# Layer 1's own rows scattered by rank in layer 0 and loaded plainly, in a four-layer graph network on one core

## The chip, the cores and the metric

The kernel runs on one core of one Trainium2 chip. Times are device microseconds (us) of that core. The core has five engines that run side by side, each with its own in-order queue: TensorE (PE, matrix products and transposes), VectorE (DVE), ScalarE (ACT), GpSimd (POOL) and SyncE (SP, which here only issues transfers). ACT and SP issue plain transfers; POOL issues the indirect ones, gathers and scatters whose row numbers lie in memory. An engine that waits for a semaphore holds back everything behind it in its own queue.

## The reference, cut to what matters

There are N = 2708 nodes with 128 features each, and a 2708 x 2708 adjacency matrix in which some 16 entries per row are not zero. Four layers follow one another, each ending in a residual sum and a layer norm. Layers 0 and 1 matter here:

```python
# layer 0
msg = H.T @ X;  inv_deg = 1 / H.sum(axis=0)          # H = adj
x = layernorm(x + msg * inv_deg[:, None])
# layer 1
s = x @ msg_w[:, :D].T
d = x @ msg_w[:, D:].T
messages = gelu(s[:, None, :] + d[None, :, :] + msg_b)
aggregated = einsum('ijd,ij->id', messages, adj)
h = gelu(concat([x, aggregated]) @ upd_w.T + upd_b) + x
x = layernorm(x + layernorm(h))
```

Layer 2 is `adj @ (x @ W)` with a norm over the nodes, layer 3 an attention over the neighbours in four heads.

## The kernel before

The nodes form 22 blocks of 128 rows (the last has 20). Since the matrix is sparse, layer 1 and layer 3 don't work on it whole but on lists: per node up to 31 neighbours with their values, and the node's own entry of the diagonal.

**First stage, making the lists.** SP loads the rows of adjacency, 1354 KB per block, into a ring of nine buffers (`load`, L388). For each block PE accumulates layer 0's product (`count_and_sum`, L400), then POOL clears the diagonal entry in the tile, ACT counts the entries (a Sign pass with accumulation, L416), and DVE finds the entries, segment by segment, with 8-wide maximum and index searches (`extract`, L420). Four weights of layer 1 are loaded and transposed at L679 (`weight`, L369), after nine blocks have been taken in the program's order.

`lists` (L514) decodes what the search found. A found place is a number of which the low 8 bits are the column within a segment, and the bits above, counted backwards, the candidate's number. The decoding makes columns and values of it, on DVE, and copies the count, the node number and the diagonal beside them.

**Ranks.** Nodes are then sorted by their count of neighbours, so that blocks of 128 sorted nodes have lists of like length (`CAPS`, L44: 30 messages for the first block down to 8). There are two groups: blocks 0 to 12 and blocks 13 to 21. `ranking(g)` (L478) makes a key per node, transposes it, writes it to DRAM, reads it back broadcast to all partitions, and lets ACT run one Sign pass per block whose accumulated sum says how many keys are greater. `ranked(g)` (L507) turns the sums into row numbers on DVE. `place` (L546) scatters the lists by these ranks to `lists_dram`, and `sorted_lists` (L558) loads them back in sorted order, with `perm`, the node that stands at each sorted place, and `idx`, the neighbours' row numbers.

**Layer 0's end.** `layer0` (L722) normalises four blocks at a time (five such quads, and two single blocks), as a pipeline of generators that yield between steps. It leaves `x` in `xs`, multiplies it by the weight of `d`, and writes `x` and `d` in natural node order to the two halves of `dx_dram`, 256 floats a row, with two plain transfers on SP per quad.

**Layer 1.** For each sorted block, in the order `TURNS`, `own_row` (L808) gathers the block's own rows of `dx_dram` by `perm`, one block ahead, into `x_s`, of which there are three buffers. `messages` (L816) computes `s` from it, and for each list position gathers 128 rows of 512 bytes (`msg`, L844), seen as a table of twice as many half rows, which is why `idx` is doubled at L569. DVE adds `s`, ACT applies Gelu, DVE weighs and sums. There are five `msg` buffers of up to eight positions. `update` (L860) finishes the block; L881 is the last that reads `x_s`. Its result is scattered to `x2_dram`.

Beside this, blocks 13 to 21 are still searched, and all blocks are transposed (`transposed`, L898): PE transposes, ACT copies to `at_sb` (three buffers), SP writes to `at_dram`. From the twelfth block on, layer 2's product takes rows of `at_dram`, gathered by `perm` (`layer2`, L942). `load3` (L577) loads lists for layer 3 on SP, and `spread` (L597) lays them out.

**What sets the order.** A planner orders each engine's instructions and puts in all waits; program order is the priority. Up to L799 DVE keeps the order in which the program is written (`manual_schedule`); later work may be put between. Each queue is then fixed, and runs as its waits allow.

```python
            x_s = mine.tile([P, 2, D], FP, name="x_s", bufs=3)
            gather(
                x_s[0:n].rearrange("p t d -> p (t d)"), dx_dram, perm[0:n, b : b + 1]
            )
```

Of the kernel before, what the change touches and what calls it, by code (L numbers as in the profile page):

```python
# [9 lines left out]
FP = mybir.dt.float32  # L10
AF = mybir.ActivationFunctionType
ALU = mybir.AluOpType
# [73 lines left out]
def gnn_resnorm_kernel(  # L86
# [124 lines left out]

    dx_dram = tables.tile([NBLK * P, 2 * D], FP, name="dx_dram")
# [30 lines left out]
    def gather(dst, table, index, rows=N):  # L243
        nc.gpsimd.indirect_dma_start(  # L244
            out=dst,
            out_offset=None,
            in_=table[0:rows, :],
            in_offset=bass.IndirectOffsetOnAxis(ap=index, axis=0),
        )
# [84 lines left out]
    with ExitStack() as layer:  # L334
# [22 lines left out]
        nc.gpsimd.iota(places_i, pattern=[[-256, CAND]], base=256 * CAND, channel_multiplier=0)  # L357
# [11 lines left out]
        def weight(src, name):  # L369
            raw = small.tile([P, P], FP, name="raw_w")  # L370
            nc.scalar.dma_start(raw, src)
# [142 lines left out]
        def lists(b0, b1):  # L514
# [8 lines left out]
            nc.vector.tensor_copy(rows[:, :, 2 * SLOTS], cnt[:, b0:b1])  # L523
            nc.vector.tensor_copy(rows[:, :, 2 * SLOTS + 1], node[:, b0:b1])
            nc.vector.tensor_copy(rows[:, :, 0], diag[:, b0:b1])
            nc.vector.tensor_copy(rows[:, :, SLOTS], node[:, b0:b1])
            nc.vector.tensor_copy(code, k2[:, b0:b1, 0 : SLOTS - 1])
            nc.vector.tensor_scalar(low, code, 255, None, ALU.bitwise_and)
            nc.vector.tensor_scalar(seg, code, 8, None, ALU.arith_shift_right)
            nc.vector.tensor_scalar(seg, seg, -1.0, float(CAND), ALU.mult, ALU.add)  # L530
            nc.vector.tensor_scalar(seg, seg, 3, None, ALU.arith_shift_right)
            nc.vector.tensor_scalar(seg, seg, float(NSEG - 1), 0.0, ALU.min, ALU.max)
            cols = rows[:, :, SLOTS + 1 : 2 * SLOTS]
            nc.vector.scalar_tensor_tensor(cols, seg, float(SEGW), low, ALU.mult, ALU.add)
            nc.vector.tensor_scalar(cols, cols, float(N - 1), 0.0, ALU.min, ALU.max)
            nc.vector.scalar_tensor_tensor(cols, v1, 0.0, cols, ALU.is_gt, ALU.mult)
            nc.vector.tensor_scalar(
                seg, seg, float(SPAN), float(127 - TOP), ALU.mult, ALU.add
# [19 lines left out]
        def sorted_lists(g):  # L558
# [3 lines left out]
            for c0, c1, n in parts:  # L562
# [6 lines left out]
                nc.vector.tensor_scalar(  # L569
                    idx[0:n, c0:c1, :], ls[0:n, c0:c1, SLOTS : 2 * SLOTS], 2.0, None, ALU.mult  # L570
                )
# [150 lines left out]
        def layer0(b0, count, n):  # L722
# [31 lines left out]
            nc.vector.reciprocal(v, v)  # L754
            for j in range(count):
                nc.vector.tensor_scalar(
                    xs[0:n, b0 + j, :], h[0:n, j, :], sums[:, j : j + 1], v[:, j : j + 1],
# [3 lines left out]
            nc.sync.dma_start(  # L761
                dx_dram[b0 * P : b0 * P + w, D : 2 * D].rearrange("(b p) w -> p b w", p=n),
# [1259 lines left out]
```

## Time and profile before

| what | value |
|---|---|
| median of 3 runs | 1965.46 us (1963.5 to 1975.81) |
| the profiled execution | 1612.16 us, span 1610.4 us |
| mean granted PE clock in it | 0.708 |
| busy PE, DVE, ACT, POOL (of the span) | 73%, 73%, 43%, 56% |
| own-row gathers (`x_s`), POOL | 22, 950 ns each |
| message gathers (`msg`), POOL | 368, 950 ns each |
| gathers of `at_dram`, POOL | 22, 948 ns each |

The profile is of one execution, the table's median of three others. A row of the profile gives the line in the kernel, the engine, the operation, what it writes and reads, how often it ran, its busy time and mean duration, and then the engine's idle time just before it with what ended that. "issue" means that the profile shows no releaser.[...] In the page, the span falls into making the lists (to about 170 us), layer 0's end (to about 205 us), layers 1 and 2's product (to about 840 us), the norm and tables (to about 905 us), and layer 3.

### The profile page before, as it was taken

The numbers are of one execution on the slowest core, as the hardware profiler recorded it, in microseconds if no ns is written. First come the engines' busy times: TensorE is split into PE (matmuls) and PEld (weight loads), VectorE is DVE, ScalarE is ACT, GpSimd is POOL, SyncE is SP. The second block draws the span as 40 slices with busy tenths as digits, with TensorE's granted clock in tenths as the row PEclk, the third lists the DMA queues.
The fourth block names the chain that finished last, engine by engine and source line by source line (L and its number), as shares of the span: only waits on it lengthen the run. The fifth ranks groups of instructions, "written<-read, shape, count | busy, mean of one in ns | idle before, by whom it ended". The sixth has DMA issues, their size and how long they took to land. (4 is left out here: it accounts for less than half of the span.)

```text
span 1610.4 us, 23528 instructions
## 1 busy us (share of the span) xinstructions
PE 1170.0 (73%) x5771; PEld 827.4 (51%) x5771; DVE 1182.0 (73%) x5376; ACT 697.6 (43%) x2670; POOL 897.8 (56%) x996
## 2 busy tenths in 40 slices
PE   6996333555357536666896689988888988998994
PEld 6896323344246435565783234544554545555553
DVE  7999967888356554444547398897888888888883
ACT  3448467655235311111115244544444555455442
POOL 1001167777667577765613577665656656676521
PEclk9898655655556677677678766776787778767675
DMA  8733368888358734343333779875766766877630
GB/s 273 286 141 127 94 186 201 246 248 237 101 136 215 224 77 164 128 169 140 104 109 121 245 229 225 234 223 159 221 204 198 209 187 166 230 199 215 186 92 8
DMA packets 164685, 288.21 MB, mean 179 GB/s; under 512 B 46610, under 2 KB 118512, under 8 KB 157439
## 3 DMA queue, kind: packets, MB, share of 16 engines
q0 software_dynamic: 60496, 190.76, 40.9%
q1 hardware_dynamic: 95923, 90.91, 18.1%
q10 hardware_dynamic: 8120, 4.95, 1.2%
q8 instruction: 48, 0.79, 0.2%
q14 instruction: 98, 0.80, 0.2%
HBM read 242.50 MB, written 43.97 MB: 178 GB/s over the span
## 5 line engine op out<-in xcount | busy, mean ns | idle before, releaser
L244 POOL DMA_INDIRECT g<-t_dram,idx x400 | 403.6, 1009 | 189.3 <-issue 141.1
L244 POOL DMA_INDIRECT msg<-dx_dram,idx x368 | 349.7, 950 | 119.1 <-issue 93.9
L1314 ACT ACTIVATE sum_junk<-g 126x128 bf16<-126x128 f32 (+3 forms) x800 | 235.2, 295 | 115.8 <-DVE g L1306 63.4
L1283 PE MATMUL z<-x,copies 32*126 32x512 f32 (+3 forms) x800 | 210.8, 875 | 33.1 <-DVE g L1483 32.3
L949 PE MATMUL acc<-x_nat,at_rows 128*128 128x128 f32 (+2 forms) x968 | 151.0, 319 | 83.1 <-DMA at_rows<-at_dram,perm 82.7
L923 PE MATMUL pt_a<-ident,rows 128*128 128x128 f32 (+2 forms) x475 | 110.1, 388 | 133.6 <-ACT at_sb L928 132.3
L949 PEld LDWEIGHTS acc<-x_nat,at_rows 128*128 128x128 f32 (+2 forms) x968 | 138.0, 226 | 93.2 <-DMA at_rows<-at_dram,perm 75.9
L1483 DVE TENSOR_TENSOR g<-g,z 126x1536 f32<-126x1536 f32 (+3 forms) x100 | 174.8, 1748 | 11.7 <-PE z L1283 11.2
L1288 PE MATMUL z<-g,ident 126*126 126x512 f32 (+3 forms) x200 | 164.7, 918 | 0.0
L923 PEld LDWEIGHTS pt_a<-ident,rows 128*128 128x128 f32 (+2 forms) x475 | 80.2, 200 | 156.4 <-ACT at_sb L928 152.6
L1314 ACT ACTIVATION_READ_ACCUMULATOR sum_junk<-g 126x1 f32 (+3 forms) x800 | 149.5, 187 | 0.0
L835 DVE SCALAR_TENSOR_TENSOR own<-msg,ls,own 128x128 f32<-128x128 f32 (+1 forms) x302 | 105.4, 349 | 56.1 <-ACT msg L853 53.5
L1360 PEld LDWEIGHTS po_s<-wm,g 126*128 126x128 f32 (+3 forms) x800 | 118.6, 232 | 42.1 <-DVE wm L1347 32.7
L1360 PE MATMUL po_s<-wm,g 126*128 126x24 f32 (+6 forms) x800 | 120.5, 305 | 25.0 <-DVE wm L1347 23.3
L405 PE MATMUL acc<-x_nat,rows 128*128 128x129 f32 (+3 forms) x1012 | 130.5, 291 | 11.2 <-DMA rows<-in_adj_dram 11.2
L405 PEld LDWEIGHTS acc<-x_nat,rows 128*128 128x128 f32 (+2 forms) x1012 | 125.2, 201 | 16.2 <-DMA rows<-in_adj_dram 11.7
L1306 DVE SCALAR_TENSOR_TENSOR g<-g,a_ps 126x1024 f32<-126x1024 f32 (+3 forms) x100 | 121.1, 1211 | 0.0
L435 DVE MAX8 cv<-rows 128x8 f32<-128x247 f32 (+2 forms) x242 | 95.5, 400 | 6.7 <-POOL rows L395 6.7
L1288 PEld LDWEIGHTS z<-g,ident 126*126 126x126 f32 (+3 forms) x200 | 40.6, 254 | 116.3 <-issue 89.7
L1283 PEld LDWEIGHTS z<-x,copies 32*126 32x126 f32 (+3 forms) x800 | 63.7, 239 | 70.6 <-DVE g L1483 27.0
L430 DVE FIND_INDEX8 ci<-cv,rows 128x8 uint32<-128x247 f32 (+2 forms) x242 | 98.4, 407 | 0.0
L1298 DVE SCALAR_TENSOR_TENSOR g<-z,a 126x128 f32<-126x128 f32 (+3 forms) x400 | 91.7, 284 | 2.3 <-PE z L1288 0.9
(297 smaller groups left out, 2093.2 us busy)
## 6 DMA issues: line engine op xcount, KB each, us to landing
rows<-in_adj_dram SPq DMA_DIRECT2D x34, 1354.0 KB
at_dram<-at_sb SPq DMA_DIRECT2D x105, 256.0 KB
g<-t_dram,idx POOLq DMA_INDIRECT x400
msg<-dx_dram,idx POOLq DMA_INDIRECT x368
t_dram<-t_row SPq DMA_DIRECT2D x21, 256.0 KB
at_dram<-at_sb SPq DMA_DIRECT2D x21, 64.0 KB
dx_dram<-x_nat SPq DMA_DIRECT2D x5, 256.0 KB
dx_dram<-d_sb SPq DMA_DIRECT2D x5, 256.0 KB
```

The source lines that it names most:

```text
L244: nc.gpsimd.indirect_dma_start(out=dst, out_offset=None, in_=table[0:rows, :], in_offset=bass.IndirectOffsetOnAxis(ap=index, axis=0),)
L405: nc.tensor.matmul(accs0[k][0:m, c0 : c0 + f1 - f0], lhsT=rows[0:n, j0 : j0 + m], rhs=x_nat[0:n, b, f0:f1], start=k not in started, stop=( ...
L430: nc.vector.max_index(out=ci[0:n, at], in_max=cv[0:n, at], in_values=rows[0:n, c0 : c0 + cw])
L835: nc.vector.scalar_tensor_tensor(to, m, v, last, ALU.mult, ALU.add)
L923: nc.tensor.transpose(pt[0:m, j, 0:n], rows[0:n, c0 : c0 + m], ident[0:n, 0:n])
L949: nc.tensor.matmul(accs2[ib // 4][0:m, (ib % 4) * D : (ib % 4 + 1) * D], lhsT=at[0:n, i0 : i0 + m], rhs=xw[0:n, b, :], start=(k == 0 and i ...
L1283: nc.tensor.matmul(z3[0:e, r, :] if r < 3 else z1[0:e], lhsT=copies[g][rows, j, :], rhs=own[b][1][rows, :], start=True, stop=r < 3, skip_g ...
L1288: nc.tensor.matmul(z1[0:e], lhsT=ident[0:e, 0:e], rhs=g4[0:e, 3, 0:HD], start=False, stop=True, skip_group_check=True,)
L1306: nc.vector.scalar_tensor_tensor(z, z, 0.0, a_ps[0:e].unsqueeze(1).to_broadcast((e, 2, HD)), ALU.max, ALU.mult)
L1314: nc.scalar.activation(junk[0:e], g4[0:e, r, hd * D : (hd + 1) * D], AF.Identity, accum_out=sc[0:e, r, hd : hd + 1],)
L1360: nc.tensor.matmul(po[:, p0 * HEADS : (p0 + g) * HEADS], lhsT=g4s[i][0:e, r, HD : HD + D], rhs=wm[0:e, 4 * i + r, :, :], start=True, stop= ...
L1483: nc.vector.tensor_tensor(z, z, z3[0:e], ALU.add)
```

## The change

- `layer0` writes its result into a new tile `dx`, which holds `d` and `x` of a node side by side, three buffers for quads and two for single blocks. It no longer writes `xs`. `d` alone goes to a new table `d_dram` in natural order, by a plain transfer on SP; `d` and `x` together are scattered by rank to `dx_dram`, 128 rows of 1 KB per scatter, 22 in all, declared independent of one another.
- For that, `ranking(1)` moves ahead of layer 0 and `ranked(1)` into its middle. A quad that reaches beyond block 12 waits for it before it scatters.
- `own_row` becomes a plain load on SP, since `dx_dram` is now in sorted order. Messages are gathered from `d_dram`; `idx` isn't doubled any more.
- `lists`: the offset of the places is chosen so that one shift by 11 gives the segment; 16 operations on DVE become 9, and four small copies go to ACT.
- The four layer-1 weights are loaded on SP's queue, not on ACT's.

```diff
+    d_dram = tables.tile([NBLK * P, D], FP, name="d_dram")
...
-        nc.gpsimd.iota(places_i, pattern=[[-256, CAND]], base=256 * CAND, channel_multiplier=0)
+        nc.gpsimd.iota(places_i, pattern=[[-256, CAND]], base=256 * (CAND + 7), channel_multiplier=0)
...
             raw = small.tile([P, P], FP, name="raw_w")
-            nc.scalar.dma_start(raw, src)
+            nc.sync.dma_start(raw, src)
...
-            nc.vector.tensor_copy(rows[:, :, 2 * SLOTS], cnt[:, b0:b1])
-            nc.vector.tensor_copy(rows[:, :, 2 * SLOTS + 1], node[:, b0:b1])
-            nc.vector.tensor_copy(rows[:, :, 0], diag[:, b0:b1])
-            nc.vector.tensor_copy(rows[:, :, SLOTS], node[:, b0:b1])
+            for at, of in ((0, diag), (SLOTS, node), (2 * SLOTS, cnt), (2 * SLOTS + 1, node)):
+                nc.scalar.copy(rows[:, :, at], of[:, b0:b1])
             nc.vector.tensor_copy(code, k2[:, b0:b1, 0 : SLOTS - 1])
             nc.vector.tensor_scalar(low, code, 255, None, ALU.bitwise_and)
-            nc.vector.tensor_scalar(seg, code, 8, None, ALU.arith_shift_right)
-            nc.vector.tensor_scalar(seg, seg, -1.0, float(CAND), ALU.mult, ALU.add)
-            nc.vector.tensor_scalar(seg, seg, 3, None, ALU.arith_shift_right)
-            nc.vector.tensor_scalar(seg, seg, float(NSEG - 1), 0.0, ALU.min, ALU.max)
+
+            nc.vector.tensor_scalar(seg, code, 11, None, ALU.arith_shift_right)
             cols = rows[:, :, SLOTS + 1 : 2 * SLOTS]
-            nc.vector.scalar_tensor_tensor(cols, seg, float(SEGW), low, ALU.mult, ALU.add)
-            nc.vector.tensor_scalar(cols, cols, float(N - 1), 0.0, ALU.min, ALU.max)
+            nc.vector.scalar_tensor_tensor(cols, seg, float(-SEGW), low, ALU.mult, ALU.add)
+            nc.vector.tensor_scalar(
+                cols, cols, float(NSEG * SEGW), float(N - 1), ALU.add, ALU.min
+            )
...
             nc.vector.reciprocal(v, v)
+            dx = brief.tile([P, count, 2, D], FP, name=f"dx{count}", bufs=3 if count > 1 else 2)
             for j in range(count):
                 nc.vector.tensor_scalar(
-                    xs[0:n, b0 + j, :], h[0:n, j, :], sums[:, j : j + 1], v[:, j : j + 1],
+                    dx[0:n, j, 1, :], h[0:n, j, :], sums[:, j : j + 1], v[:, j : j + 1],
                     ALU.add, ALU.mult,
                 )
             w = (count - 1) * P + n
-            nc.sync.dma_start(
-                dx_dram[b0 * P : b0 * P + w, D : 2 * D].rearrange("(b p) w -> p b w", p=n),
-                xs[0:n, b0 : b0 + count, :],
-            )
             yield
...
-            d_sb = brief.tile([P, 4, D], FP, name="d_sb")
-            nc.scalar.copy(d_sb[0:n, 0:count], pm[0:n, 0:count])
+            nc.scalar.copy(dx[0:n, :, 0, :], pm[0:n, 0:count])
             nc.sync.dma_start(
-                dx_dram[b0 * P : b0 * P + w, 0:D].rearrange("(b p) w -> p b w", p=n),
-                d_sb[0:n, 0:count],
-            )
-
+                d_dram[b0 * P : b0 * P + w, :].rearrange("(b p) w -> p b w", p=n),
+                dx[0:n, :, 0, :],
+            )
+            while b0 + count > SPLIT and 1 not in known:
+                yield
+            for j in range(count):
+                did = scatter(
+                    dx_dram, rank[0:n, b0 + j : b0 + j + 1],
+                    dx[0:n, j].rearrange("p t d -> p (t d)"),
+                )
+                for before in known[1:]:
+                    tc.declare_no_dep(
+                        did, before, query=mybir.DependencyQuery.ANY_SYNC,
+                        reason="each row has a place of its own",
+                    )
+                known.append(did)
+
+
+        known = [0]
         running = []
+        ranking(1)
         for quad in [(NFULL, 1, NREM), *quads()[:-1]]:
             running.append(layer0(*quad))
             for steps in reversed(list(running)):
                 if next(steps, "done") == "done":
                     running.remove(steps)
+        ranked(1)
+        known[0] = 1
         while running:
...
         sorted_lists(0)
-        ranking(1)
...
             x_s = mine.tile([P, 2, D], FP, name="x_s", bufs=3)
-            gather(
-                x_s[0:n].rearrange("p t d -> p (t d)"), dx_dram, perm[0:n, b : b + 1]
+            nc.sync.dma_start(
+                x_s[0:n],
+                dx_dram[b * P : b * P + n, :].rearrange("p (t d) -> p t d", t=2),
             )
...
-                    gather(
-                        msg[0:n, k, :], dx_dram.rearrange("n (t d) -> (n t) d", t=2),
-                        idx[0:n, b, c0 + k + 1 : c0 + k + 2], rows=2 * N,
-                    )
+                    gather(msg[0:n, k, :], d_dram, idx[0:n, b, c0 + k + 1 : c0 + k + 2])
...
-                    if e == SPLIT:
-                        ranked(1)
```

## The prediction

> **What bounds the kernel now.** I read the stretches of 25 us first: VectorE (DVE) is full from 25 to 175 us, GpSimd (POOL) from 205 to about 810 us, TensorE (PE) and DVE together after 925 us. The change acts in the first two. Next came the groups by line; the columns are busy us, mean ns of one, then the engine's idle time before them and what ended it.
>
> ```profile
> L244 POOL DMA_INDIRECT msg<-dx_dram,idx x368 | 349.7, 950 | 119.1 <-issue 93.9 <-DMA msg<-dx_dram,idx 8.4 <-ACT back L908 2.9
> L244 POOL DMA_INDIRECT x_s<-dx_dram,perm x22 | 20.9, 950 | 65.1 <-issue 36.3 <-ACT junk L502 27.6 <-PE pt_a L923 0.6
> L252 POOL DMA_INDIRECT lists_dram<-lists,rank x22 | 21.5, 978 | 20.4 <-DVE spread L604 6.0 <-issue 5.2 <-DVE deg L706 4.8
> ```
>
> One gather takes 0.95 us and POOL starts the next 0.30 us later. A full POOL therefore shows 19 busy us in 25, and that is what the stretches from 225 to 400 us and from 575 to 700 us show (17.0 to 19.1). Layer 1 is paced by POOL at 1.25 us per gather. The own-row gathers are few but have much idle time ahead of them. The timelines of POOL and of DVE show where it lies:
>
> ```profile
> 705.59 0.94 POOL L244 DMA_INDIRECT at_rows<-at_dram,perm  x1 [0.30 <-issue]
> 706.84 1.00 POOL L252 DMA_INDIRECT x_dram<-x_n,perm  x1 [0.30 <-DVE spread L604]
> 708.14 0.96 POOL L244 DMA_INDIRECT at_rows<-at_dram,perm  x1 [0.30 <-issue]
> 717.39 0.92 POOL L244 DMA_INDIRECT x_s<-dx_dram,perm  x1 [8.29 <-issue]
> ...
> 747.19 0.95 POOL L244 DMA_INDIRECT x_s<-dx_dram,perm  x1 [7.42 <-issue]
> ```
> ```profile
> 716.27 0.29 DVE L881 SCALAR_TENSOR_TENSOR new<-new,x_s 128x128 f32<-128x128 f32 x1 [1.91 <-ACT new L880]
> ...
> 746.15 0.29 DVE L881 SCALAR_TENSOR_TENSOR new<-new,x_s 128x128 f32<-128x128 f32 x1 [1.92 <-ACT new L880]
> ```
>
> Each stalled own-row gather starts about 1 us after L881, the last reader of an older `x_s`. Of three buffers none is free, and POOL, which works in order, stands with the next block's messages queued behind. It is a ring: POOL's `at_rows` gathers, their landing, PE's products ahead of the update's, L881, POOL again. Such stalls stand at 561.95 (6.65 us), 717.39 (8.29), 747.19 (7.42) and 772.53 (9.64), together 32.0 us.
>
> The start, in the timelines of PE, POOL and DVE:
>
> ```profile
> 15.21 0.45 PE L373 MATMUL pt_w<-ident,raw_w 128*128 128x128 f32 x1 [15.21 <-DMA raw_w<-in_L_gnn_msg_w_dram]
> 16.16 0.29 POOL L395 TENSOR_SCALAR_AFFINE_SELECT rows<-rows 128x128 f32<-128x128 f32 x1 [11.97 <-DMA lnw<-in_L_gnn_ln_w_dram]
> 16.49 0.74 DVE L435 MAX8 cv<-rows 128x8 f32<-128x247 f32 x2 [6.70 <-POOL rows L395]
> ```
>
> PE's first instruction is the transpose of a weight, issued on ScalarE's (ACT's) queue at 11.12 us behind the features. The products of block 0, the clearing of its diagonal and DVE's search all stand behind it. Last, the waits (us in total, times, longest), of SyncE's queue (SP) and of DVE:
>
> ```profile
> SPq L583 <- DMA lists_dram<-lists,rank: 29.7, 1, 29.7
> ...
> DVE to L619 <- DMA node<-lists_dram: 27.1, 2, 25.6
> ```
>
> SP works in order too: from 412.9 to 442.6 us it stood at one load, and DVE stood 25.6 us for another behind it. This matters because the change gives SP more to wait for.
>
> **The Trainium skill.** "DMA: Bandwidth & Descriptors", section "Queues, rings and completion order": on each DMA engine a queue's descriptors are consumed in ring order, and the engine alternates between queues. So a weight on SP's queue comes behind the adjacency rows issued before it; no row of this trace shows a weight there. The same page, "Anatomy of one DMA — SWDGE (gpsimd) path": a DMA's semaphore wait is spent on the sequencer that issues it, and a DMA has about 2.0 us of fixed cost. The trace agrees: the write of `key_dram` is issued at 197.78 us and the read that waits for it at 200.20. "Perfetto Trace Analysis", section "DMA Instruction — SWDGE (GPSIMD)": POOL's interval is descriptor generation, not the movement of data. It agrees: a gather of 10.8 KB rows (`at_rows`, 0.948 us) costs POOL what one of 512-byte rows does (0.950).
>
> **Part by part.** The profiled execution took 1612.16 us, of which 1610.4 are span. The median of the runs is 1965.46, 353 us longer, and nothing in the page shows where. I sum against 1612.16 and carry the result to the median in microseconds, unscaled, since POOL and queues pace what changes. (Scaled by 1.219 it would be a fifth more.)
>
> *Weights on SP's queue.* The four loads leave ACT. On SP they come after nine row loads, so I expect their transposes to fall behind the products of those blocks on PE. PE then starts when rows 0 and the first features are in. DMA moved 2.3 MB by 8 us (43, 256, 414 and 418 GB/s in four stretches of 2 us) and 3.0 MB by 10; two row tiles and three feature blocks are 3.0 MB, so about 10 us. DVE's own set-up ends at 9.8. DVE starts near 10.3 instead of 16.49: -6 us. DVE is full up to 175 us, so this goes through. Bounds: -7; and +22 if the weight stays first on PE but lands behind nine row tiles of 1.39 MB (12.5 MB at 321 GB/s, the mean of the first 60 us, is 39 us). The later two loads wait on SP for a free raw buffer, about to 65 us, with row loads queued behind them. Today the tenth is issued at 38.3 and its search begins near 98, so I cost that at nothing.
>
> *Lists in nine operations.* Per call three integer operations go (starts 150.35 to 151.28, 0.93 us) and four small copies move to ACT (149.17 to 149.45, 0.28 us). That is 1.2 us for seven blocks and about 0.9 for six: -2.1 us on full DVE before layer 0. The two later calls lie under POOL's pace: nothing. ACT gets 0.8 us per call (four at 0.19, the row of `var`); the lists' scatters wait for that, and their reload isn't used before 194 us. The changed base of the codes and the plain index copy cost nothing.
>
> *Ranking group 1 early.* Nine Sign passes of 1044 columns (1.17 + 0.19 us, 12.1 us in all) move from 204 to 226 us, where they lay under POOL's gathers, into layer 0. The chain is key at 174, write and broadcast about 7 us, passes from 181. ACT had 6.3 us of idle time from there to 200.5: +5.8 us if nothing else stretched. DVE stands at `ranked(1)` for the last pass, with the normalising of quads queued behind.
>
> *Scatters by rank.* 22 scatters at 1.27 us (the row of `lists_dram`) are 28 us of POOL time, in a stretch where POOL idles from 178 to 205. Seven plain writes on SP go. But the new tile `dx4` has three buffers for five quads, and a buffer is free only when its scatters have landed. The first quad's `d` is copied at 188.5; four scatters are 5.1 us, landing 2: 195.6, where the fourth quad's scaling starts at 190.46 today. The second: 192.6, POOL busy until 198.7, landed 200.7, where the fifth quad's scaling starts at 192.43: +8.3 us. DVE waits in order, layer 1's searches behind it. The passes partly overlap these waits. I take +11 us for both until the first message gather (208.0 us today), POOL's remaining scatters included. Bounds: +6 and +20.
>
> *Own rows on SP.* Two of the 22 gathers stood ahead of the first message and are inside that +11. Eleven up to 530 us at 1.25 us are 13.8; DVE is 85% busy there and DMA 0.8 to 0.9, so I take -10 (0 to -14). Nine later: -11.3. The slot stalls leave POOL. PE is then next late: 16.1 and 13.7 busy us in 25 between 700 and 750 are 18 in a cycle of 29.8, against POOL's 21. I take half, -16 (0 to -31). The plain loads are issued one block ahead; five message buffers hold some 40 gathers, 50 us, which hides a late own row. If that cover is gone, POOL stands as before. Message gathers from `d_dram` read the same 512-byte rows: nothing.
>
> Sum: -6 - 2.1 + 11 - 10 - 11.3 - 16 = -34.4 us. The profile would be 1578 us, the median 1931 us.
>
> **Rivals.** *The gain is hidden.* Layer 0 costs +20 (passes and buffers added), and PE's wait for `at_rows` (82.7 us in nine waits) replaces the slot stalls: -6 - 2 + 20 - 10 - 11 is -9, so 1956. For it: those waits are there already. Against it: they end sooner when POOL issues sooner.
>
> *SP stands in line: slower.* Own-row loads wait on SP for an `x_s` buffer, and the first for all 22 scatters. Behind them stand the `at_dram` writes and adjacency loads. With writes late, the three `at_sb` buffers fill, ACT stops in its copies (it waits 32.6 us for those writes today), Gelu and L881 come later, and so does the buffer. Price: 5 us in each of 12 blocks before 530 us, +60 - 34 = +26: 1991. It decides from 2.9 us per block (34/12). For it: the 29.7 us stand. Against it: SP mostly waits for ACT at its writes (152 us), so it has slack.
>
> *The weight stays first on PE:* +22 in place of -6, so -6 in all: 1959. Against it: nine row loads of the same queue arrive before it.
>
> **Numbers.** Likeliest 0.55: 1931, its own range 1905 to 1946. Hidden 0.20: 1956. SP 0.18: 1991. Weight 0.07: 1959. About 1% (19.7 us) is what a measurement of this kernel can tell from no change. Of the likeliest, 0.53 are faster by over 1%; of hidden and weight, 0.05, and 0.03 are slower. Faster 0.58, same 0.24, slower 0.18. Range 1902 to 1985: up to half of SP's case, and the low end is the sum with all slot stalls gone and the first half in full.
>
> **What would show it.** Right: DVE's first MAX8 near 10 us; POOL's own-row gathers gone and no idle over 5 us between the block's last `at_rows` and the next message; first message gather near 211 us (219 less the 8 before it). Wrong: pt_w still PE's first; SP's waits at the own-row load over 3 us per block with writes behind; POOL still idle 7 us per block late in layer 1, now for something else.

## The result and the profile after

Beside each other on one chip, the kernel before took 1971.90 us (median of 12 runs, 1963.50 to 1982.36) and the changed one 1974.23 us (12 runs, 1964.51 to 1983.05). The ratio is 0.9992, 95% interval 0.9968 to 1.0016: no difference. Forecast were 1931 us, a ratio of 0.982.

One thing has to be known for all numbers that follow: the time of this kernel depends on the chip. On some chips the kernel before takes about 1625 us (I call them short), on others about 1970 us (long); the profile of before was taken on a short chip, the runs of both kernels and the profile of after on long ones. A ratio is therefore always to the kernel before on the same chip, and stages are compared between profiles of the same sort of chip.

The profiled execution of the changed kernel took 1977.24 us, of which 1975.5 are span. Its start, from the timeline of all engines (start, duration, engine, line, what, and in brackets the idle time before it and what ended it):

```profile
10.91 9.29 PE L406 MATMUL acc<-x_nat,rows 128*128 128x129 f32 x66 [10.91 <-DMA x_nat<-in_x_dram]
...
12.08 0.74 DVE L436 MAX8 cv<-rows 128x8 f32<-128x247 f32 x2 [2.27 <-POOL rows L396]
```

The weights' transpose is no longer PE's first instruction, and DVE's search begins at 12.08 us in place of 16.49. The other end of the start, POOL's timeline:

```profile
170.38 0.96 POOL L253 DMA_INDIRECT lists_dram<-lists,rank  x1 [0.30 <-issue]
196.90 0.96 POOL L253 DMA_INDIRECT dx_dram<-dx,rank  x1 [25.57 <-ACT dx L773]
198.16 0.96 POOL L253 DMA_INDIRECT dx_dram<-dx,rank  x1 [0.30 <-DVE k L467]
...
227.01 0.96 POOL L253 DMA_INDIRECT dx_dram<-dx,rank  x1 [0.30 <-issue]
230.94 0.98 POOL L245 DMA_INDIRECT msg<-d_dram,idx  x1 [2.97 <-DVE ka L471]
```

POOL still idles to 196.90, then runs all 22 scatters in a row, and only behind the last of them gathers its first message, at 230.94 us. It did that at 208.00 before. What kept POOL idle stands in ACT's timeline:

```profile
177.04 1.17 ACT L503 ACTIVATE junk<-key_row,nkey 128x1044 int8<-128x1044 f32 x1
178.11 0.18 ACT L503 ACTIVATION_READ_ACCUMULATOR junk<-key_row,nkey 128x1 f32 x1
178.21 0.38 ACT L743 ACTIVATE ln_junk<-h,sums 128x128 bf16<-128x128 f32 x1
178.50 0.19 ACT L743 ACTIVATION_READ_ACCUMULATOR ln_junk<-h,sums 128x1 f32 x1
178.59 1.15 ACT L503 ACTIVATE junk<-key_row,nkey 128x1044 int8<-128x1044 f32 x1
...
196.03 0.59 ACT L773 COPY dx<-pm_d 128x512 f32<-128x512 f32 x1
```

The nine Sign passes of the early ranking (L503) lie one by one between the Squares of the first quads (L743), so the first full quad's `d` is copied at 196.03 us. Behind 230.94 us the profiles of before and after can't be compared, since they are of two sorts of chip. The groups by line of after show what the long chip does:

```profile
L245 POOL DMA_INDIRECT msg<-d_dram,idx x368 | 348.0, 946 | 266.5 <-issue 209.7 <-ACT at_sb L936 41.2 <-ACT back L916 10.4
...
L253 POOL DMA_INDIRECT x_dram<-x_n,perm x22 | 21.9, 994 | 134.0 <-DVE own L846 64.3 <-DVE x_n L319 52.4 <-DVE spread L601 14.3
...
L253 POOL DMA_INDIRECT dx_dram<-dx,rank x22 | 21.2, 963 | 35.4 <-ACT dx L773 25.6 <-issue 4.9 <-DVE kb L460 3.8
```

A message gather costs POOL what it did (946 ns), but there are 266.5 us of idle time before them, and 134.0 before the scatters of the updates, which wait for DVE. The own-row gathers are gone, and 22 scatters of nearly the same price (963 ns) have come.

### The profile page after: what moved, and what is told of

The parts are those of the page before. It is cut to its first block, busy times and chain, and to the rows that moved or that the text cites. A ratio compares the mean times of both kernels' runs of the same rounds, so it can differ in the third digit from the quotient of the medians.

```text
span 1975.5 us, 23576 instructions
## 1 busy us (share of the span) xinstructions
PE 1274.4 (65%) x5771; PEld 887.3 (45%) x5771; DVE 1190.2 (60%) x5348; ACT 701.0 (35%) x2686; POOL 894.6 (45%) x996
## 5 line engine op out<-in xcount | busy, mean ns | idle before, releaser
L245 POOL DMA_INDIRECT msg<-d_dram,idx x368 | 348.0, 946 | 266.5 <-issue 209.7
L1289 PE MATMUL z<-x,copies 32*126 32x512 f32 (+3 forms) x800 | 229.2, 938 | 64.6 <-issue 26.3
L957 PE MATMUL acc<-x_nat,at_rows 128*128 128x128 f32 (+2 forms) x968 | 165.7, 330 | 62.3 <-issue 48.8
L931 PE MATMUL pt_a<-ident,rows 128*128 128x128 f32 (+2 forms) x475 | 115.4, 401 | 128.1 <-ACT at_sb L936 93.9
L957 PEld LDWEIGHTS acc<-x_nat,at_rows 128*128 128x128 f32 (+2 forms) x968 | 147.8, 235 | 76.9 <-issue 64.1
L1294 PE MATMUL z<-g,ident 126*126 126x512 f32 (+3 forms) x200 | 174.7, 970 | 0.0
L1366 PE MATMUL po_s<-wm,g 126*128 126x24 f32 (+6 forms) x800 | 139.7, 333 | 43.4 <-DVE wm L1353 41.6
L1366 PEld LDWEIGHTS po_s<-wm,g 126*128 126x128 f32 (+3 forms) x800 | 137.9, 265 | 62.0 <-DVE wm L1353 48.1
L931 PEld LDWEIGHTS pt_a<-ident,rows 128*128 128x128 f32 (+2 forms) x475 | 85.6, 209 | 149.5 <-ACT at_sb L936 107.3
```

The source lines that it names most:

```text
L245: nc.gpsimd.indirect_dma_start(out=dst, out_offset=None, in_=table[0:N, :], in_offset=bass.IndirectOffsetOnAxis(ap=index, axis=0),)
L931: nc.tensor.transpose(pt[0:m, j, 0:n], rows[0:n, c0 : c0 + m], ident[0:n, 0:n])
L957: nc.tensor.matmul(accs2[ib // 4][0:m, (ib % 4) * D : (ib % 4 + 1) * D], lhsT=at[0:n, i0 : i0 + m], rhs=xw[0:n, b, :], start=(k == 0 and i ...
L1289: nc.tensor.matmul(z3[0:e, r, :] if r < 3 else z1[0:e], lhsT=copies[g][rows, j, :], rhs=own[b][1][rows, :], start=True, stop=r < 3, skip_g ...
L1294: nc.tensor.matmul(z1[0:e], lhsT=ident[0:e, 0:e], rhs=g4[0:e, 3, 0:HD], start=False, stop=True, skip_group_check=True,)
L1366: nc.tensor.matmul(po[:, p0 * HEADS : (p0 + g) * HEADS], lhsT=g4s[i][0:e, r, HD : HD + D], rhs=wm[0:e, 4 * i + r, :, :], start=True, stop= ...
```

## The experiments

Stages are read from POOL's timeline throughout: the first message gather; from there to the last gather of `at_rows` ("the gathers"); from there to the first instruction of layer 3 ("the tail"); and the rest.

**The kernel before, profiled again** (no edit), on a short and on a long chip.

> The kernel before, unchanged, profiled again. The profile of before took 1612 us and its timed runs 1963 to 1982, the profile of the changed kernel 1977. If the profile of before was an outlier of that one execution (theory A: in the runs that count both kernels lose about 350 us to stalls that POOL's pace in that profile doesn't contain), this profile takes 1960 to 1985 us, its layer 3 as long as the changed kernel's (about 785 us against 695), and its POOL has over 200 us of idle time ahead of the message gathers. If profiling itself made the kernel before quick (theory B), it takes about 1612 again.

> The kernel before, profiled on the chip of this call. On a chip of about 1970 us: first message gather at 208 as on the others (nothing differs before it), the gathers of layers 1 and 2 then last about 790 us in place of 600, and layer 3 about 140 us longer. On a chip of about 1627 us: the stages of the earlier profile within 2%.

The first took 1631.56 us, the second 1982.28. The outlier theory of the first expectation falls: the profile of before was an ordinary run of a short chip. Stages in us:

```
                     first message  gathers  tail   rest    span
before, short (e1)       208.0       611.6   94.2   715.8  1629.7
after,  short (e5)       231.4       569.7  104.1   711.5  1616.7
before, long  (e13)      210.2       804.6  111.9   853.7  1980.4
after,  long  (e15)      232.4       778.4  113.3   851.2  1975.2
```

Before the first message the two sorts of chip agree within 2.2 us. (One start varies as much by itself: e4 below changes only what comes later, and its first message came at 210.10 us on the chip of e1. So 2 us of difference there mean nothing.) Of the extra 351 us of the kernel before, 193 lie in the gathers and 138 in layer 3, whose 400 gathers are POOL's as well.

**The changed kernel again** (no edit), on a short and on a long chip.

> The changed kernel, unchanged, timed beside the kernel before on a chip that need not be the first one's. If the chip is one on which the kernel before takes about 1627 us: with its own rows on POOL the changed kernel took 1.008 there, and five own-row buffers alone were worth 31 us; the plain loads take 22 gathers off POOL (27 us) besides the stalls. Theory B (POOL's pace counts there, and layer 0's cost is about 20 us): 0.985 to 0.995. Theory A (no gain from POOL anywhere): 1.0 to 1.01. If the chip is one on which the kernel before takes about 1970 us: 0.999 again.

> The changed kernel once more, for the comparison in this call: 0.999 on a chip of about 1970 us, 0.9945 on one of about 1627.

Short: 0.9945 (0.9926 to 0.9963), the upper end of theory B. Long: 1.0012 (0.9985 to 1.0040), as in the result. The table is the ledger: the first message comes 22 to 23 us later on both; the gathers are shorter by 41.9 us on the short chip and by 26.2 on the long one; the tail gives back 9.9 and 1.4.

**One part of the change: weights on SyncE's queue** (short chip).

```
-            nc.scalar.dma_start(raw, src)
+            nc.sync.dma_start(raw, src)
```

> The kernel before with the four weight loads on SyncE's queue, nothing else changed. Prediction: DVE's first search near 10 us in place of 16.5 and 6 us less in all, ratio 0.997. Theory A: the first 6 us come as predicted (DVE is full to 175 us in both profiles), but they need not reach the end: ratio 0.995 to 1.0. Against it: 1.0 or above, if the loads on SyncE hold up the adjacency rows behind them.

0.9964 (0.9947 to 0.9980), the 6 us forecast. DVE's first search began at 11.95 us. The first message gather came at 207.56, only 0.4 us earlier than in e1, so the profile doesn't show these 6 us where the prediction had them: the number came, its path didn't.

**One suspected cost: the own rows' buffers** (short chip; the kernel before, then the changed one).

```
-            x_s = mine.tile([P, 2, D], FP, name="x_s", bufs=3)
+            x_s = mine.tile([P, 2, D], FP, name="x_s", bufs=5)
```

> The kernel before with five buffers for the own rows in place of three, so that POOL never stands at an own-row gather for a free buffer; nothing else changed. As the prediction's term for the slot stalls has it, 16 us less (0 to 31): ratio 0.984 to 1.0, likeliest 0.992. Theory A: these stalls were on the path only in the quick profile; ratio 0.997 to 1.003.

> The changed kernel with five own-row buffers in place of three; nothing else changed. If SyncE stands at an own-row load for a free buffer and holds the writes behind it (rival: SP in line), 10 us or more come back: ratio at least 0.006 below that of the changed kernel in the same call. If the plain loads are hidden, as the prediction has it: within 0.003 of it.

In the kernel before: 0.9812 (0.9779 to 0.9845), 31 us for two buffers, all that the stalls held. In the changed kernel: 0.9937 (0.9917 to 0.9957) beside 0.9945, so nothing. SP does stand at the own-row loads for a free buffer (159.4 us in eleven waits on the short chip, 162.0 in the profile of after), but five buffers take only part of that away (115.3 us in eight waits are left), so this run alone doesn't settle the rival of SP in line. The next one does, on a short chip; neither was run on a long one.

**Own rows back on POOL** (short chip): the plain load undone, all else as changed.

```
-            nc.sync.dma_start(
-                x_s[0:n],
-                dx_dram[b * P : b * P + n, :].rearrange("p (t d) -> p t d", t=2),
-            )
+            gather(
+                x_s[0:n].rearrange("p t d -> p (t d)"), dx_dram, node_i[0:n, b : b + 1]
+            )
```

> The changed kernel with its own rows gathered by POOL again (22 gathers, from the table in rank order), all else as changed. Theory A (layer 1 isn't paced by POOL in the runs that count): ratio to the kernel before within 1% of 1, as the changed kernel's 0.999. Theory B (taking the gathers from POOL gained what I predicted, 37 us, and the start of layer 1 lost it): 1.01 to 1.02. Theory C (the plain load's wait on SyncE costs what the gathers gained): 0.98 to 0.99.

1.0082 (1.0054 to 1.0110), theory B. Against the changed kernel's 0.9945 (two chips, each with its own kernel before) the plain loads are worth 1.4%, 22 us, where the rival of SP in line had them cost more than they gain. The gathers' stretch is 589.1 us against 569.7. What remains of the change without them is 13 us slower than before.

That remainder shows one thing more. Its gathers' stretch is 22.5 us shorter than the 611.6 of e1, though POOL gathers the own rows as before, into three buffers:

```profile
L245 POOL DMA_INDIRECT x_s<-dx_dram,node_i x22 | 21.0, 956 | 20.6 <-issue 8.6 <-DMA at_dram<-at_sb 6.8 <-PE own L834 4.6
```

The idle time for issue is 8.6 us in place of 37.5 (e1): most of the stalls at the buffers had gone before the loads moved to SP.

**Five buffers for the quads in layer 0** (short chip).

```
-            dx = brief.tile([P, count, 2, D], FP, name=f"dx{count}", bufs=3 if count > 1 else 2)
+            dx = brief.tile([P, count, 2, D], FP, name=f"dx{count}", bufs=5 if count > 1 else 2)
```

> The changed kernel with five buffers for the quads' tiles in layer 0 in place of three (the scratch of the zero degrees shares an older tile's place, to make room); nothing else changed. The prediction had the scaling of the fourth and fifth quad wait 5 and 8 us for scatters; then 5 to 8 us come back, ratio 0.003 to 0.005 below the changed kernel's. If POOL's 22 scatters in a row set the first message instead, nothing comes back: within 0.002.

0.9917 (0.9895 to 0.9939) beside 0.9945 (0.9926 to 0.9963): the intervals overlap. The last `d` was copied at 210.83 us in place of 215.42, and the first message came at 227.31, 4.1 earlier. The wait shows in the profile, a little under the size expected; in all it isn't clear of noise.

**The early ranking alone**, in the kernel before, with three own-row buffers (short chip) and with five (long chip).

```
         running = []
+        ranking(1)
         for quad in [(NFULL, 1, NREM), *quads()[:-1]]:
...
-        ranking(1)
```

> The kernel before with the ranking of group 1 (three small operations on VectorE, a transpose, a copy, two DMAs and nine Sign passes on ScalarE) ahead of layer 0 in place of behind it; nothing else changed. Prediction: 5.8 us later at the end of layer 0, for ScalarE has 6.3 us of idle time there and the passes are 12.1; ratio 1.0036 if it goes through, 1.0 if POOL's or DVE's work hides it.

> The kernel before with group 1 ranked ahead of layer 0 and five own-row buffers. With three buffers the early ranking cost nothing in all (0.999), though it put the first message gather 11 us later and the whole order of layer 1's instructions changed with it, the stalls at the own rows' buffers gone. If the 11 us are real and were only covered by the gain of those stalls: 0.9812 + 0.0066 = 0.988. If an early ranking is hidden: 0.981.

With three buffers 0.9992 (0.9967 to 1.0016): nothing in all. Yet the first message came at 218.77 us, 10.8 later, and its groups by line show what covered that:

```profile
L244 POOL DMA_INDIRECT x_s<-dx_dram,perm x22 | 21.0, 953 | 51.5 <-DVE cv L435 38.4 <-issue 6.8 <-PE own L824 5.0
```

The idle time for issue before own-row gathers fell from 37.5 us (e1) to 6.8: the stalls at the buffers are gone, though there are three as before. Moving one call changed the order that the planner gives POOL in the whole of layer 1 (x_s gathers stand at other places among the messages), and the gathers lasted 582.3 us in place of 611.6. The tail gave 10.0 us of it back (104.2 us). With five buffers, on a long chip, 1.0201 (1.0159 to 1.0244), where 0.988 was expected: the first message came at 219.51, and the gathers lasted 832.5 us. No theory here had that; see the next run.

**The kernel before with weights, lists and five buffers**, so the two small parts of the change, and buffers in place of its scatters, early ranking and plain loads (two long chips, one short).

```
...
-            nc.scalar.dma_start(raw, src)
+            nc.sync.dma_start(raw, src)
...
-            nc.vector.tensor_copy(rows[:, :, 2 * SLOTS], cnt[:, b0:b1])
...
+            for at, of in ((0, diag), (SLOTS, node), (2 * SLOTS, cnt), (2 * SLOTS + 1, node)):
+                nc.scalar.copy(rows[:, :, at], of[:, b0:b1])
...
-            x_s = mine.tile([P, 2, D], FP, name="x_s", bufs=3)
+            x_s = mine.tile([P, 2, D], FP, name="x_s", bufs=5)
```

> The kernel before with the change's two small parts (weights on SyncE's queue, lists in nine operations) and five own-row buffers; own rows still gathered by POOL, nothing ranked early, nothing scattered in layer 0. If the parts add: 0.9812 for the buffers, 0.0036 for the weights, 2 us of 1627 (0.0013) for the lists: 0.976, and better than the changed kernel's 0.9945 by 30 us. If the time that POOL gains is lost again behind layer 1 (the last gather to the end took 810 us in the kernel before and 816 in the changed one): 0.98 to 0.985.

> The kernel before with weights on SyncE's queue, lists in nine operations and five own-row buffers. It was 0.995 on a chip of about 1970 us. On one of about 1627 us, where five buffers alone gave 0.981 and the weights 0.996: 0.976, so faster than the changed kernel by 1.5 to 2%. On a longer chip: 0.995 again, within 0.5% of the changed kernel.

> The kernel before with weights on SyncE's queue, lists in nine operations and five own-row buffers: 0.976 on a chip of about 1627 us, where five buffers alone gave 0.981; 0.994 to 0.995 on one of about 1970, as twice before.

Short: 0.9787 (0.9752 to 0.9822), so the parts nearly add. Long: 0.9951 (0.9928 to 0.9974) and 0.9939 (0.9908 to 0.9970), the latter beside the changed kernel's 1.0012 on the same chip. It beats both kernels on both sorts of chip. Its first message came at 203.33, 205.58 and 205.97 us, and its gathers lasted 797.5 us (e9) where the same layer 1 in another order lasted 832.5 (e12, one profile of each; the ranking's place and the decoding of the lists differ besides): on a long chip the order can be worth some 35 us.

**The changed kernel without scatters** (long chip): seven plain writes in their place. The ordering by rank is left out, so the own rows loaded later are other nodes'.

```
-            while b0 + count > SPLIT and 1 not in known:
-                yield
-            for j in range(count):
-                did = scatter(
...
+            nc.sync.dma_start(
+                dx_dram[b0 * P : b0 * P + w, :].rearrange("(b p) w -> p b w", p=n),
+                dx[0:n].rearrange("p b t d -> p b (t d)"),
+            )
```

> The changed kernel with its 22 scatters replaced by seven plain writes on SyncE's queue, so that POOL does nothing in layer 0. It leaves out the ordering by rank: the own rows that layer 1 then loads are other nodes'. The first message gather stood at 231 us in the changed kernel, behind 22 scatters from 197 on. Theory D (the scatters set the start: 28 us of them, of which only some 8 lie before the last write of the message table lands): first gather near 211, 20 us less in all, ratio 0.982. If the early ranking alone holds layer 0 up (it put the first gather from 208 to 219 in the kernel before): first gather near 220, ratio 0.988. If the message table's last write is what counts: 228 or later, ratio 0.993.

```profile
219.11 0.99 POOL L245 DMA_INDIRECT msg<-d_dram,idx  x1 [45.97 <-DMA at_dram<-at_sb]
```

First message at 219.11 us, the second of the three cases: ahead of it the early ranking holds the start up, and the scatters, with the waits for the quads' buffers, add another 12 to 13 (230.94, or 232.4 in e15). In all 0.9932 (0.9906 to 0.9957), where this case was put at 0.988; that is 12 to 16 us under the changed kernel's 0.9992 and 1.0012 on other long chips, as much as the start gained.

**Scatters and plain loads for group 0 alone** (long chip): blocks 13 and up are gathered by POOL from a table in the nodes' order, with five own-row buffers, and ranked behind layer 0.

```
-            while b0 + count > SPLIT and 1 not in known:
-                yield
             for j in range(count):
+                if b0 + j >= SPLIT:
+                    continue
...
+            nc.sync.dma_start(
+                nat_dram[b0 * P : b0 * P + w, :].rearrange("(b p) w -> p b w", p=n),
...
+            if b >= SPLIT:
+                gather(x_s[0:n].rearrange("p t d -> p (t d)"), nat_dram, perm[0:n, b : b + 1])
+                return x_s
```

> The changed kernel with its own path for group 0 alone: 13 scatters by rank and 13 plain loads; the nine blocks of group 1 are written in the nodes' order and gathered by POOL as before, with five own-row buffers, and group 1 is ranked behind layer 0 as before. Theory D: 13 scatters (16.5 us) fit into POOL's idle time ahead of the message table, first gather 200 to 212 us; 13 gathers (16 us) are gone from layer 1: ratio 0.972, below the kernel before with five buffers and weights. If POOL's pace isn't the bound in the first half (DVE is 80% busy there): as that one, 0.976 to 0.98.

1.0098 (1.0064 to 1.0132): slower, against both cases. The scatters ran early as meant, the first at 188.32 us and the last at 206.37, but the first message came at 216.32, for between 193.4 and 206.1 SP had no write of `d` to issue, and the gathers lasted 817.0 us, 20 more than in e9, with 13 fewer. This design isn't the way out.

**Passes behind the quads' work** (short chip), with five buffers for the quads.

```
         running = []
-        ranking(1)
         for quad in [(NFULL, 1, NREM), *quads()[:-1]]:
...
+        ranking(1)
         ranked(1)
```

> The changed kernel with the ranking of group 1 behind the six quads' steps in place of ahead of them, and five buffers for the quads' tiles; scatters, plain loads and the rest as changed. If the passes' place between the quads' Squares costs the start: the first full quad's d is copied near 186 us again in place of 196, POOL's scatters start near 187, 22 of them end near 216, first message gather near 217 in place of 231, 10 to 14 us less in all: ratio 0.992 on a chip of about 1970 us, 0.987 on one of about 1627. If the scatters of group 1 then wait for the passes: first gather 222 to 228, ratio within 0.003 of the changed kernel with five buffers (0.9917 on the shorter chip).

POOL's timeline:

```profile
185.49 0.96 POOL L253 DMA_INDIRECT dx_dram<-dx,rank  x1 [14.52 <-ACT dx L773]
...
200.69 0.96 POOL L253 DMA_INDIRECT dx_dram<-dx,rank  x1 [0.30 <-issue]
211.06 0.88 POOL L253 DMA_INDIRECT dx_dram<-dx,rank  x1 [9.41 <-DVE var L751]
...
225.98 0.98 POOL L245 DMA_INDIRECT msg<-d_dram,idx  x1 [2.87 <-DVE k L467]
```

The 13 scatters of group 0 now start 11 us earlier, at 185.49, so the passes' place had cost that. But the nine of group 1 wait for their ranks, the messages stand behind them, and the first one comes at 225.98. 0.9968 (0.9948 to 0.9987): not better than the changed kernel, and worse than e7's 0.9917 with the same five buffers, on another short chip.

**No message gathers** (long chip): the messages of layer 1 loaded plainly, the same bytes. The gathering is left out, so the rows are not the neighbours'.

```
-                for k in range(kc):
-                    gather(msg[0:n, k, :], d_dram, idx[0:n, b, c0 + k + 1 : c0 + k + 2])
+                b1 = c0 % 13
+                nc.sync.dma_start(
+                    msg[0:n, 0:kc, :],
+                    d_dram[b1 * P : (b1 + kc) * P, :].rearrange("(k p) d -> p k d", p=P)[0:n],
+                )
```

> The changed kernel with the messages of layer 1 loaded plainly on SyncE's queue, one load per buffer of up to eight messages, the same bytes in the same 512-byte rows. It leaves out the gathering: the rows are not the neighbours'. Theory E (POOL's gathers slow the other engines on the longer chips): VectorE, ScalarE and TensorE have no idle time for issue or remote in layer 1 any more, while layer 3, whose gathers stay, keeps its own; on a longer chip layer 1 falls by 300 us or more, to what it takes on a shorter one. Theory F (the bytes or the transfers do it): the idle time stays, and layer 1 takes 650 us or more there. On a shorter chip both have layer 1 at 350 to 500 us, paced by VectorE (its busy time from 230 to 800 us is about 330) and TensorE.

1706.58 us (two runs) beside 1971.39 of the kernel before and 1972.43 of the changed one, a ratio of 0.8653 (0.8611 to 0.8694) to the former. Layer 3 began at 853.4 us in place of 1124.0, 271 earlier; layer 3 itself, whose gathers stayed, took 852.6, where the changed kernel took 851.2. What theory E looked for is in the waits from 230 to 700 us (total, times, longest), first of the changed kernel on the same chip, then of this one:

```profile
ACT new L888 <- remote: 43.1, 4, 17.6
...
DVE spread L601 <- remote: 39.8, 4, 15.7
...
PE pt_a L931 <- issue: 25.9, 10, 10.4
```
```profile
PEld tail L902 <- issue: 8.0, 2, 6.5
...
DVE to L616 <- issue: 2.9, 2, 1.8
...
ACT x_nat L907 <- issue: 0.6, 1, 0.6
```

With the gathers the engines stand tens of microseconds for nothing that the profile shows; without them that is gone. So it goes with POOL's gathers, not with the number of bytes, and theory F falls. (The order of the rows and the queue that carries them changed too, so POOL's own work and its queue's transfers aren't told apart.) (The gain is 271 us and not the 300 expected, since the tail grew to 203 us.)

## Why the prediction was wrong

**The start: this is the step that failed.** I had the first message near 211 us: 208, plus 11 for layer 0, less 8 for weights and lists. It came at 230.9 to 232.4.

- *Ranking group 1 early* was put at 5.8 us, on the argument that ACT had 6.3 us of idle time for passes of 12.1. That argument takes idle time for granted wherever it lies. The passes stand ahead of the first quads' copies in ACT's order, so the first full quad's `d` came later by all of them: at 200.00 us in e8 against 187.87 in e1. In the first message it measured 10.8 us (e8), and 13 to 16 between e9, e16 and e10, which differ in more.
- *Scatters by rank* were put at the waits for the three quad buffers, 8.3 us, with passes and waits overlapping to 11 together. The waits measured 4.1 us (e7). POOL's remaining scatters were said to be in the 11, but no working stands for them. By the prediction's own times, the first scatter starts at 188.5 less 8, so at 180.5, and the last of 22 ends at 208.5. But a quad's scatters start only when its `d` is copied, and the first started at 196.90; the idle time that I had given them from 178 on was of no use up to there. (With the passes behind the quads it was 185.49, e17.) What reaches past the table's readiness then stands ahead of every message. In all the scatters cost 12 to 13 us at the first message, the buffers' waits included (e10). So the two costs don't overlap to 11, they add up to some 23.
- A scatter's landing was put at 2 us, checked on the write of `key_dram`, which is a plain transfer that ACT issues. Behind the last scatter POOL idled 2.97 us in the profile of after, and 6.78 in e5, before the first message. The quads' tiles are closed (L808) before the message buffers are opened (L812), so probably the first gather waits for the scatters to land before it may use their memory; no run tests it.
- Weights and lists gave 2 to 7 us at the first message (203.3 to 206.0, against 208.0 and 210.2), not 8. DVE's search began at 12.08 and not 10.3, and "DVE is full up to 175 us, so this goes through" failed behind the lists: DVE came to layer 0 at 162.82 us in e18, where it was 170.13 in e1, and then stood for ACT's squares:

```profile
173.23 0.14 DVE L749 TENSOR_SCALAR var<-var 20x1 f32<-20x1 f32 x1 [3.88 <-ACT ln_junk L744]
```

Replace the 3 us of this step by the 23.4 measured, and a sum of -34.4 becomes -14; the short chip's profiles stand 13.0 apart. That this comes so near is in part luck: the gathers gained 41.9 us where the other terms had 37.3, the tail lost 9.9, and the rest gained 4.3.

**The own rows on SP: right in mechanism and size, on a short chip.** -21.3 us forecast for the gathers, 22 measured (e2 against e5). **Slot stalls: real, but the term was too small and the way they went another.** I took half of 32 us because PE seemed next late; five buffers alone returned 31 us (e4). PE was not. But in the changed kernel the stalls didn't go for my reason, that the loads leave POOL: with the gathers back on POOL most of them were gone already (e2), as they were when one call had moved (e8). And the two terms don't add: the gathers became 41.9 us shorter, not 53. A new wait has come, in the timelines of POOL and of DVE (e5):

```profile
577.41 1.00 POOL L253 DMA_INDIRECT x_dram<-x_n,perm  x1 [16.96 <-DVE x_n L319]
```
```profile
570.72 0.15 DVE L616 CAST to<-node 128x1 int32<-128x1 f32 x1 [8.51 <-DMA node<-lists_dram]
```

POOL stands 16.96 us at an update's scatter (4.8 in e1), and half of that is DVE's own wait for a load of layer 3's lists, with the update behind it. All four short profiles with plain own-row loads have it (16.8 to 17.4 us), and e2 doesn't (7.1 at most); whether the loads bring it or the order that came with them is open. Another 9.9 us came back in the tail. All six short-chip kernels that rank group 1 before layer 0 is done have a tail of 102 to 104 us, the four others 94 to 95. That this is the planner's order of the last blocks is argued, not shown.

**Carrying the sum to the median: the second step that failed.** I carried microseconds from a short chip to long runs since nothing in the page showed where the rest lay. Part of it lies in the very stretch that the change shortens. There POOL's pace is not what sets the time. The lines of e13, and of e16 with five buffers on the same chip, show it:

```profile
L252 POOL DMA_INDIRECT x_dram<-x_n,perm x22 | 21.9, 993 | 59.1 <-DVE x_n L318 39.6 <-DVE own L835 10.9 <-DVE spread L604 4.2
...
L244 POOL DMA_INDIRECT x_s<-dx_dram,perm x22 | 20.8, 946 | 171.6 <-issue 74.9 <-ACT junk L502 29.3 <-PE own L824 25.1
```
```profile
L252 POOL DMA_INDIRECT x_dram<-x_n,perm x22 | 21.9, 995 | 131.0 <-DVE x_n L318 60.2 <-DVE own L833 57.5 <-DVE spread L602 10.0
...
L244 POOL DMA_INDIRECT x_s<-dx_dram,perm x22 | 21.0, 954 | 69.3 <-DVE k L466 36.7 <-DVE cv L435 8.2 <-issue 8.0
```

The buffers took 102.3 us of idle time from the own-row gathers; 71.9 came back before the updates' scatters, which wait for DVE, and 31.2 before the messages. The stretch became only 9.6 us shorter. The change met the same: the gathers shrank by 26.2 us where the short chip gave 41.9, and with the start's 22.2 that leaves 5.2 us between the profiles, tail and rest included, and none between the runs.

**The rivals.** "The gain is hidden" had its first half right (layer 0 at +20; the start measured +22 to +23), and its total, -9, is the short chip's 0.9945. Its second half, a wait of PE for `at_rows` in place of the slot stalls, wasn't what took the gain: that wait was 73.4 us in e5 and 82.9 in e1. SP in line is excluded by e2 as the outcome on the short chip, since the plain loads gain 22 us there; that SP's queue has a part in the new wait of 16.96 us is not excluded. The weight is not first on PE.

**What was to show it.** Own-row gathers gone from POOL: right. No idle over 5 us between the last `at_rows` and the next message: wrong on both sorts of chip. On the short one the 16.96 us stand just there; only from 600 to 798 us has POOL no idle time above 4 us. First message near 211: wrong, and that alone would have told.

## What to carry to other kernels

A gather replaced by a scatter does not relieve POOL, which paid 963 ns for the one and 950 for the other, so ask when the first of the moved operations can start and what is queued behind the last. Idle time counts for moved work only if it lies behind the work that others wait for. And try the cheap remedy for a stall first: on the short chip two more buffers gave 31 us where this rewrite gave 9.

## What the runs showed of the hardware

That chips differ by 20% on one program was not expected, nor how. On a long chip other engines stand idle while POOL issues gathers back to back. Two views of the profile of after, PE's timeline and the stretches of 25 us (busy us of PE, its weight load, DVE, ACT and POOL with their instructions, then clock, DMA share, GB/s):

```profile
777.53 0.37 PE L957 MATMUL acc<-x_nat,at_rows 128*128 128x128 f32 x1 [1.72 <-issue]
779.63 0.37 PE L957 MATMUL acc<-x_nat,at_rows 128*128 128x128 f32 x1 [1.73 <-issue]
781.73 0.37 PE L957 MATMUL acc<-x_nat,at_rows 128*128 128x128 f32 x1 [1.73 <-issue]
783.83 0.37 PE L957 MATMUL acc<-x_nat,at_rows 128*128 128x128 f32 x1 [1.73 <-issue]
786.63 0.37 PE L957 MATMUL acc<-x_nat,at_rows 128*20 128x128 f32 x1 [2.43 <-issue]
```
```profile
775.00:800.00 25.00, 4.73 (x13) 2.89 (x13) 0.00 (x0) 0.00 (x0) 15.10 (x16) 0.50 0.43 150
```

PE issues one product every 2.10 or 2.80 us (once 3.50), multiples of 0.70, and the profile names nothing that it waits for; DVE and ACT wait for it and do nothing at all in these 25 us, while POOL keeps its 1.25 us per gather until its buffers are full. Summed over the 200 longest rows of the waits, the idle time put down to issue or remote is 388 us for ACT, 275 for DVE and 151 for PE (e15), against 70, 0 and 1 on a short chip (e5). Taking the message gathers away ends it in layer 1.

Two rivals can be read off the profiles of the kernel before. Here is its gathers' stretch in the same columns, on a short chip (e1) and on a long one (e13):

```profile
208.00:819.60 611.60, 349.24 (x1792) 293.75 (x1793) 355.48 (x1670) 225.96 (x476) 416.14 (x438) 0.62 0.60 168
```
```profile
210.20:1014.80 804.60, 382.16 (x1775) 309.48 (x1776) 357.09 (x1665) 222.88 (x471) 415.34 (x438) 0.60 0.44 129
```

Slower work isn't it: DVE, ACT and POOL are busy as long on both, and PE, at a granted clock of 0.60 against 0.62, 33 us longer, while the stretch is 193 us longer. Slower transfers aren't it either: the packets of POOL's queue took 41.8% of the 16 engines' span in e1 and 33.1% in e13, so 681 and 656 us. What in the chip ties these engines to POOL's gathers, why only some chips do it, and why one order of the same work suffers 35 us more than another, stays open; these runs can't separate it further.
